# Two levels of seven products for queries and keys, over pairs of batches, with inner weight sums loaded for each pair

## The chip, the cores and the metric

The kernel runs on one core of one Trainium2 chip. The metric is the device time of one execution in microseconds. The core has five engines with a queue of instructions each: TensorE (PE in the profile, its weight loads PEld), VectorE (DVE), ScalarE (ACT), GpSimd (POOL) and SyncE (SP), which issues nearly all transfers. Each engine takes its instructions in order; between engines there are semaphores. 16 DMA engines carry the transfers. All data is fp32.

## The reference

For 64 batches of 256 tokens with 512 features, two layers are computed, each with a residual sum and a normalization over the features:

```python
deg = jnp.sum(adj, axis=-1, keepdims=True)
agg = jnp.einsum('bij,bjf->bif', adj, x) / jnp.maximum(deg, EPS)
out = relu(jnp.einsum('bnf,of->bno', concatenate([x, agg], axis=2), W))   # layer 0
x = _layernorm(x + out)

q, k, v = proj(Wq, bq), proj(Wk, bk), proj(Wv, bv)                         # layer 1, 8 heads of 64
scores = einsum('bhqd,bhkd->bhqk', q, k) * SCALE * (adj + adj)
ctx = einsum('bhqk,bhkd->bhqd', softmax(scores), v)
x = _layernorm(x + ctx @ Wo.T + bo)
```

The weights W are 512 x 1024, the four weights of layer 1 are 512 x 512.

## The kernel before

**Work and names.** The work of a batch is cut into small steps, each a function under a short name; a word such as `L35+2` in a plan means step L35 for batch 2i+2. The names that matter here:

- Dzx, xT: x is loaded in blocks and turned, features to partitions. xS: its sums for the outer level. Ls: sums for the inner level, in small tiles xs. L and Le: products of the first layer and what takes them out of PSUM.
- Dadj, Dza, aT, deg: the adjacency matrix, its turned copy, its row sums. Y, Yk, Yj: neighbours' product and its taking out. Dx, AYr, AYb, AYp, AYn: the rows of x, the residual sum, and the first normalization.
- Dway, Dz1, x1T, yS: the result goes through DRAM and comes back turned; sums of it. Q, V: queries and keys, values; Qk, Qj, Vk, Vj take them out.
- For each of four pairs of heads a to d: S (scores, two 64-row products side by side), m (mask and maximum), M, e, f (exponentials), r, n (normalize), T, Dw, Ds (turned on VectorE and through DRAM), C (context, two 64-column products side by side), c (copied).
- cS, O, Ok, Oj: output product and what takes it out. Drest, bo: the residual with bias. lb, lp, ln, Dout: the last normalization and the store.

**Seven products.** A product of two matrices cut in two each way is made of seven products of sums of blocks instead of eight (`winograd`, L461). Three accumulators a, b and c (banks of PSUM) collect them, and products are added onto what was already taken out. So of product 6 the sum goes onto product 1's bank after `k1` has read it. The first layer (L, `split_product`, L527) does this twice over: the outer level over a pair of batches, with seven outer products, each again of seven, 49 products of 128x256 for a pair. `W0_inner` holds the inner sums of the weights for good. Batches 0 and 1 use one level (P, `multiply_first`, L583). Queries and keys (`multiply_q`, L615) use one level for each batch: seven steps of eight products of 128x128. Values and output (`right_weights`, L498) use one level for each batch: seven steps of two products of 128x256. Neighbours (Y): seven of 128x256.

**Order.** START, PLAN and END list all steps over all engines, in an order that a planner made ahead of time; each engine takes its instructions in the order of these lists. PLAN is one turn, for two batches: it holds the first layer of batches 2i+2 to 2i+5 beside the second of 2i-1 to 2i+2. It is run 28 times. The SyncE queue follows the same list: a transfer whose buffer isn't free holds all behind it. PSUM has eight banks, given out in turn. One tile of 256 rows is held for `x`.

Of the kernel before, what the change touches and what calls it, by code (L numbers as in the profile page):

```python
# [22 lines left out]
LAST_TURNS = 2  # L23
START = """
    Dzx:0 W0h0:0 Dzx:1 W0h1:0 xT1:0 xT0:0 xS3:0 xS1:0 W0s1:0 P1:0 Dza:0 xT1:1 P5:0 xT0:1 xS1:1 Wo:0
    Pk5:0 P5:1 P1:1 Pk5:1 xS2:1 Pk1:0 xS2:0 Dadj:1 W0s2:0 P2:0 W0i1:0 Dzx:2 P6:0 aT:0 W0s3:0 Pk6:0 xS4:0
    Dadj:0 Pk1:1 aS1:0 W0s4:0 P7:0 Pj2:0 Dx:0 P3:0 Pj7:0 Y1:0 Pj3:0 Wb:0 P4:0 W0i5:0 bS1:0 bS3:0 Y5:0
    Pk4:0 xT0:2 aS3:0 P6:1 Dza:1 aS2:0 deg:0 xS3:1 Yk5:0 bS2:0 Yk1:0 Pk6:1 Wq:0 Y6:0 Y2:0 Yk6:0 aS4:0
    bv1:0 xS4:1 Y3:0 Yj2:0 bS4:0 Y7:0 Yj7:0 Yj3:0 Y4:0 AYr0:0 P7:1 AYb0:0 Yk4:0 AYp0:0 AYr1:0 P2:1 xT1:2
    AYn0:0 AYb1:0 P3:1 Pj7:1 AYp1:0 Pj2:1 Dzx:3 bv2:0 Pj3:1 AYn1:0 aT:1 Dway:0 aS1:1 P4:1 bv3:0 bS1:1  # L30
    Wv:0 deg:1 bS3:1 Y5:1 xS1:2 Pk4:1 W0i4:0 Y1:1 WqS:0 bS2:1 Y2:1 aS2:1 Yk1:1 xS3:2 Y6:1 aS4:1 Dz1:0
    xT0:3 xT1:3 Ls11:2 aS3:1 Yk5:1 Ls12:2 Yk6:1 Dx:1 Y3:1 xS1:3 Wqs1:0 L11:2 Ls51:2 Y7:1 Le11:2 bS4:1
    L51:2 Wqs3:0 L15:2 Ls13:2 L16:2 Ls52:2 L55:2 Yj7:1 Dza:2 Le16:2 Ls53:2 Wqs2:0 Le51:2 Wvs1:0 Y4:1
    L56:2 L17:2 x1T:0 Le56:2 Wvs2:0 L12:2 L52:2 L57:2 Yj3:1 yS1:0 Yk4:1 Q1:0 Dadj:2 Yj2:1 AYr0:1 V5:0
    Qk1:0 AYb0:1 Q5:0 Vk5:0 AYr1:1 AYp0:1 AYb1:1 V1:0 yS2:0 AYn0:1 aT:2 AYp1:1 W0i3:0 Qk5:0 Q6:0 Vk1:0  # L35
    Ls14:2 AYn1:1 yS3:0 Wqs4:0 V6:0 Le15:2 Dway:1 Qk6:0 L13:2 Le17:2 yS4:0 W0i2:0 Vk6:0 L14:2 Wvs4:0
    Le55:2 Q7:0 Le14:2 Le13:2 Ls23:2 Le57:2 Ls21:2 Le52:2 Ls22:2 L21:2 Le12:2 Ls54:2 Qj7:0 L54:2 Ls24:2
    V3:0 Le21:2 Le54:2 Wvs3:0 deg:2 Dx:2 L26:2 L53:2 Le26:2 Q4:0 xS2:3 W0i6:0 aS1:2 Dz1:1 xS2:2 Le53:2
    V7:0 Qk4:0 Ls61:2 Ls63:2 L25:2 Ls62:2 L61:2 Le25:2 Ls64:2 L27:2 Le61:2 xS3:3 Q2:0 Vj3:0 Drest:0
    Le27:2 W0i7:0 L22:2 L23:2 Qj2:0 L65:2 Ls71:2 Le23:2 L66:2 L62:2 Le66:2 L24:2 Le62:2 Q3:0 Vj7:0  # L40
    Le24:2 L67:2 V4:0 Le67:2 Le65:2 L64:2 Qj3:0 Vk4:0 L63:2 xS4:2 Le64:2 Le63:2 Sd:0 Ls72:2 Le22:2 xS4:3
    Sb:0 md:0 Ls31:2 Sc:0 La12:3 mb:0 Sa:0 La12:2 L75:2 L35:2 mc:0 Ls33:2 L71:2 Md:0 V2:0 Mb:0 fd:0
    Ls74:2 ma:0 L31:2 Mc:0 Ls32:2 eb:0 L72:2 L32:2 L41:2 Le75:2 ec:0 Ma:0 Dadj:3 Le71:2 Ls73:2 L73:2
    Le31:2 aS3:2 ed:0 x1T:1 Y1:2 Wos1:0 L76:2 L36:2 fb:0 Dzx:5 Le35:2 V1:1 Ls34:2 Le36:2 Le76:2 yS1:1
    fc:0 Le73:2 L33:2 rd:0 Le72:2 L37:2 nd:0 Le33:2 L77:2 La22:2 Le32:2 Dzx:4 Q1:1 Le77:2 rc:0 Le37:2
    bS1:2 Vj2:0 nc:0 Le41:2 Ls41:2 L74:2 Ls42:2 L34:2 Le74:2 Y5:2 ea:0 rb:0 Le34:2 La22:3 L46:2 Yk1:2
    L45:2 Tc:0 nb:0 Q5:1 bS2:2 aS2:2 Le45:2 Dwc:0 Le46:2 Ls44:2 fa:0 Yk5:2 V5:1 Ls43:2 Td:0 Qk1:1 L47:2
    yS2:1 Y6:2 Le47:2 Dwd:0 L42:2 yS3:1 Vk1:1 L44:2 Le42:2 bS3:2 Q6:1 ra:0 Yk6:2 na:0 aS4:2 Tb:0 Le44:2
    V6:1 Dwb:0 Vk5:1 Ta:0 Qk5:1 Dsc:0 V2:1 yS4:1 Vk6:1 xT0:5 Y7:2 bo:0 Qk6:1 L43:2 xT0:4 V3:1 Dwa:0
    xT1:5 Q7:1 Le43:2 Yj7:2 Vj3:1 bS4:2 Dsd:0 xT1:4 Ls13:4 V7:1 Wos2:0 Y4:2 Vj7:1 Y2:2 Yk4:2 bS1:3 Q3:1  # L50
    AYr1:2 Dsa:0 Wos4:0 deg:3 Y3:2 Qj7:1 Ls11:4 V4:1 xS3:4 AYb1:2 Dza:3 xS3:5 Q4:1 Vk4:1 Vj2:1 Qj3:1
    Wos3:0 Yj3:2 Yj2:2 Q2:1 Qk4:1 xS1:5 AYr0:2 Dsb:0 AYp1:2 AYb0:2 Qj2:1 C1a:0 AYp0:2 AYn1:2 C1b:0 xS1:4
    AYn0:2 Sd:1 c1:0 Dway:2 Sa:1 md:1 Sc:1 Sb:1 aT:3 Md:1 Ls53:4 fd:1 mc:1 Ls12:4 C0a:0 aS1:3 Ls51:4
    C0b:0 ma:1 Mc:1 Ls14:4 c0:0 Y5:3 Ls52:4 Y2:3 cS1:0 Dz1:2 mb:1 O2:0 aS2:3 cS3:0 O5:0 Yk5:3 aS3:3 Dx:3
    Y1:3 Ma:1 O1:0 Mb:1 Yk1:3 fa:1 cS2:0 L51:4 Ls54:4 Ok1:0 fb:1 L55:4 Ok5:0 bS2:3 O6:0 Yj2:3 Dza:4 ed:1
    L15:4 Ok6:0 cS4:0 Y6:3 Oj2:0 Le51:4 O7:0 ea:1 Yk6:3 aS4:3 x1T:2 bS4:3 L56:4 eb:1 Y3:3 bS3:3 O3:0
    Oj7:0 yS1:2 Yj3:3 Le56:4 ra:1 Y7:3 rb:1 na:1 L52:4 Yj7:3 V5:2 AYr0:3 Le52:4 O4:0 ec:1 Oj3:0 AYb0:3
    Y4:3 nb:1 L57:4 Yk4:3 AYp0:3 L11:4 AYr1:3 V1:2 AYb1:3 yS3:2 Q1:2 Vk1:2 Le11:4 rd:1 Ok4:0 AYp1:3
    AYn0:3 lb0:0 Q5:2 Tb:1 lp0:0 AYn1:3 Le15:4 aT:4 Le55:4 Dwb:1 Qk1:2 L13:4 yS2:2 Dadj:4 Le57:4 L16:4
    Ta:1 L54:4 Le16:4 V6:2 Le54:4 xS2:4 lb1:0 nd:1 Dway:3 L53:4 xS2:5 L17:4 Dwa:1 Le53:4 Ls63:4 L12:4  # L60
    Le17:4 Ls61:4 Q6:2 fc:1 Ls62:4 Ls23:4 Dsb:1 Vk6:2 Ls21:4 rc:1 Le12:4 Vk5:2 nc:1 Le13:4 L14:4 yS4:2
    L25:4 V7:2 Ls22:4 lp1:0 Le14:4 V3:2 Qk6:2 Vj7:2 Tc:1 Ls24:4 L21:4 Dz1:3 Qk5:2 Ls64:4 L61:4 Q7:2
    Le21:4 Td:1 ln1:0 ln0:0 Dwc:1 Le61:4 V4:2 Vj3:2 Dsa:1 Le25:4 L26:4 Qj7:2 Vk4:2 L65:4 Le26:4 V2:2
    Dwd:1 L27:4 Q4:2 Dsc:1 L23:4 Qk4:2 Q3:2 Le23:4 Le65:4 L66:4 Dsd:1 L63:4 Le66:4 L62:4 deg:4 L67:4
    Q2:2 Le27:4 Qj3:2 Dout:0 Le67:4 L24:4 x1T:3 L64:4 L22:4 xS4:5 Vj2:2 C0a:1 Le63:4 Ls71:4 Le62:4 xS4:4
    C0b:1 Le24:4 Le64:4 Ls31:4 Le22:4 C1a:1 Ls72:4 Qj2:2 Ls74:4 C1b:1 La12:4 c1:1 Sa:2 Ls32:4 c0:1
    Drest:1 Sb:2 ma:2 cS1:1 Dx:4 Sc:2 Ls33:4 cS3:1 mb:2 Sd:2 Ma:2 La12:5 fa:2 L75:4 L71:4 mc:2 L35:4
    Mb:2 Ls73:4 L72:4 eb:2 aS1:4 O5:1 Dzx:7 Le71:4 yS1:3 Le75:4 ea:2 O2:1 md:2 bo:1 L76:4 fb:2 L31:4
    L73:4 Dadj:5 Le31:4 O1:1 Le76:4 Le35:4 L36:4 aS3:4 Ok1:1 L77:4 Mc:2 ra:2 L32:4 Le72:4 cS2:1 na:2
    Dzx:6 Le77:4 L41:4 Ok5:1 Ls41:4 O6:1 Le73:4 Md:2 Ls34:4 rb:2 Le36:4 ec:2 Ta:2 cS4:1 L33:4 L37:4 ed:2  # L70
    La22:4 L45:4 Le32:4 Dwa:2 O3:1 Le33:4 Le37:4 nb:2 Ls43:4 Ok6:1 L74:4 bS1:4 L42:4 Le74:4 O7:1 Le41:4
    La22:5 fd:2 Oj2:1 Oj3:1 L34:4 Oj7:1 V5:3 fc:2 Ls42:4 Le45:4 Ls44:4 rd:2 lb0:1 Y1:4 nd:2 Y5:4 Dsa:2
    Yk1:4 L46:4 aS2:4 O4:1 yS3:3 Le46:4 Le34:4 Vk5:3 L47:4 rc:2 bS2:4 Le42:4 nc:2 V1:3 Tb:2 bS3:4 Q5:3
    Le47:4 Dwb:2 Vk1:3 Yk5:4 Ok4:1 Td:2 L44:4 yS2:3 Y6:4 Q1:3 lp0:1 xT1:7 Yk6:4 Tc:2 L43:4 Qk1:3 Y7:4
    xT0:7 Dwc:2 V6:3 Le43:4 Dwd:2 Yj7:4 Q6:3 bS4:4 Dza:5 Vk6:3 ln0:1 aS4:4 Y4:4 Qk6:3 yS4:3 Y2:4 Yk4:4
    V7:3 xS1:7 Le44:4 Qk5:3 Y3:4 Dsc:2 Q7:3 Yj3:4 AYr1:4 AYb1:4 Q3:3 Dsd:2 Vj7:3 Qj7:3 lb1:1 V2:3 xT1:6
    lp1:1 Q2:3 xT0:6 aT:5 Ls13:6 Dsb:2 ln1:1 AYp1:4 Yj2:4 Q4:3 AYr0:4 aS1:5 Qj3:3 AYn1:4 Dout:1 AYb0:4
    V3:3 Qk4:3 Qj2:3 AYp0:4 V4:3 Vj3:3 deg:5 Vk4:3 Ls11:6 Sd:3 AYn0:4 bS1:5 Vj2:3 C1a:2 Ls12:6 Dway:4
    Dza:6 C1b:2 C0a:2 c1:2 md:3 C0b:2 Drest:2 Md:3 c0:2 Sa:3 xS1:6 ed:3 aS3:5 Sb:3 ma:3 cS1:2 fd:3 Sc:3
    Dz1:4 Ls14:6 Ls51:6 mb:3 Y5:5 Ma:3 Ls52:6 Y1:5 ea:3 aS2:5 O2:2 bS2:5 Dx:5 Yk1:5 fa:3 O1:2 mc:3 Mb:3  # L80
    O5:2 bo:2 Y2:5 L51:6 Yj2:5 L11:6 Yk5:5 Y6:5 Le11:6 L55:6 Le51:6 cS2:2 Ok5:2 L16:6 Ok1:2 Mc:3 L52:6
    Yk6:5 bS3:5 ec:3 L56:6 x1T:4 aS4:5 Y7:5 bS4:5 fb:3 Y3:5 Yj7:5 yS1:4 O6:2 Yj3:5 Le16:6 eb:3 cS3:2
# [76 lines left out]
def kernel(  # L159
# [912 lines left out]
```

## Time and profile before

| | |
|---|---|
| runs | 2978.38, 2980.99, 2980.94 us; median 2980.94 |
| span of the profiled execution (the page gives no other time of it) | 2979.5 us |
| TensorE busy | 2948.7 us, 99% |
| VectorE, GpSimd, ScalarE busy | 2251.9, 1864.2, 1651.0 us |
| transfers | 510.77 MB, mean 171 GB/s |
| period of a turn, from L11 to L11 | 91.29 us |

A group line shows line, engine and operation, output and inputs, shapes and count, then busy time, the mean of one, and the idle time before with what ended it. Ends of matmuls are modelled, so TensorE's prices are read from start to start. The DMA share is the busy share of 16 engines.

### The profile page before, as it was taken

Reading aid. Unit: us, or ns where it says so; the run is one execution under the profiler, and the core shown is the slowest. Engines: PE = TensorE matmul, PEld = TensorE weight load, DVE = VectorE, ACT = ScalarE, POOL = GpSimd, SP = SyncE. Lnnn points to the kernel's source line nnn. Section 1 sums busy time; section 2 is a strip of 40 time slices with the busy share of each in tenths; the row PEclk is TensorE's granted clock in tenths of the full one; section 3 lists DMA queues with packets and bytes.
Section 4 is the critical chain, followed back from the end, with each engine's and each line's share of the span. In section 5 each row is a group of like instructions: output and inputs, shape, how many; then the busy total and the mean of one; then the engine's idle time right before and its main releaser. Section 6 shows DMA issues by size and latency. Waiting matters only on the chain.

```text
span 2979.5 us, 60265 instructions
## 1 busy us (share of the span) xinstructions
PE 2948.7 (99%) x18874; PEld 2576.7 (86%) x18874; DVE 2251.9 (76%) x6302; ACT 1651.0 (55%) x5001; POOL 1864.2 (63%) x3435
## 2 busy tenths in 40 slices
PE   7999999999999999999999999999999999999998
PEld 4888898888888888888888888888888888888886
DVE  6877777777787777777777877777777777777774
ACT  2455555555564555555655645656556556555565
POOL 5756666666566566666665665756666656657553
PEclk9999999999999999999999999999999999999999
DMA  7476666765756666667656577666676665776764
GB/s 173 125 190 179 165 173 155 199 179 156 187 159 174 188 173 168 172 159 194 180 157 185 159 181 188 166 175 167 156 198 176 165 180 153 192 183 164 178 171 116
DMA packets 492573, 510.77 MB, mean 171 GB/s; under 512 B 113760, under 2 KB 391264, under 8 KB 492256
## 3 DMA queue, kind: packets, MB, share of 16 engines
q1 hardware_dynamic: 490912, 505.87, 64.7%
q8 instruction: 153, 2.51, 0.4%
q14 instruction: 164, 1.34, 0.2%
q10 hardware_dynamic: 1344, 1.05, 0.2%
HBM read 307.50 MB, written 199.23 MB: 170 GB/s over the span
## 4 chain that ended last, share of the span: by engine, by line
PE 98%; POOL 1%; DVE 1%; DMA 0%; issue 0%; ACT 0%; SPq 0%; ACTq 0%; POOLq 0%; DVEq 0%
PE Qa L619 15%; PE pc L933 8%; PE Qc L619 8%; PE Va L501 7%; PE Oa L501 7%; PE Qb L619 4%; PE Vc L501 4%; PE Ya L708 4%; PE Oc L501 4%; PE Ycb L708 3%; PE sca L816 2%; PE scc L816 2%; PE scd L816 2%; PE scb L816 2%; PE Vb L501 2%; PE Ob L501 2%
## 5 line engine op out<-in xcount | busy, mean ns | idle before, releaser
L635 ACT ACTIVATE qk<-Qa,bqk 128x128 f32<-128x128 f32 x768 | 219.0, 370 | 281.5 <-PE Qa L619 281.5
L670 POOL TENSOR_SCALAR mv<-mv 128x1 f32<-128x1 f32 x256 | 67.2, 262 | 383.7 <-DVE mv L665 252.5
L619 PEld LDWEIGHTS Qa<-x1T,Wq 128*128 128x128 f32 x2048 | 248.6, 192 | 6.8 <-issue 0.3
L619 PE MATMUL Qa<-x1T,Wq 128*128 128x128 f32 x2048 | 249.4, 275 | 0.0
L989 ACT COPY cT<-pc 128x512 f32<-128x512 f32 x126 | 70.8, 586 | 250.5 <-PE pc L933 250.4
L676 ACT ACTIVATE rest<-rest,mv 128x512 f32<-128x512 f32 x128 | 100.8, 810 | 177.3 <-POOL mv L672 177.3
L832 DVE CUSTOM_DVE_ANT_0 sc<-scc,adj 128x256 f32<-128x256 f32 x256 | 92.5, 418 | 105.1 <-PE scc L816 103.1
L676 ACT ACTIVATE x<-oy,mv 128x512 f32<-128x512 f32 x128 | 105.4, 823 | 117.6 <-POOL mv L672 115.0
L440 POOL TENSOR_TENSOR xS<-xT,xS 128x256 f32<-128x256 f32 x64 | 47.1, 737 | 195.4 <-PE L6a L554 190.8
L851 ACT ACTIVATE sc<-sc,nmaxc 128x256 f32<-128x256 f32 x256 | 127.5, 500 | 71.7 <-DMA zx<-in_x_dram 39.7
L790 POOL TENSOR_TENSOR rest<-rest,bo_sb 128x512 f32<-128x512 f32 x128 | 160.7, 1277 | 8.5 <-DMA rest<-way 8.3
L851 ACT ACTIVATE sa<-sa,nmaxa 128x256 f32<-128x256 f32 x256 | 127.0, 497 | 68.5 <-POOL nmaxa L845 63.7
L671 POOL TENSOR_TENSOR mv<-mv,neg_half 128x1 f32<-128x1 f32 x256 | 144.8, 566 | 21.3
L875 ACT ACTIVATE sb<-sb,totalb 128x256 f32<-128x256 f32 x252 | 107.4, 498 | 78.9 <-DVE totalb L863 78.9
L832 DVE CUSTOM_DVE_ANT_0 sa<-sca,adj 128x256 f32<-128x256 f32 x256 | 93.2, 421 | 74.9 <-PE sca L816 72.1
L851 ACT ACTIVATE sb<-sb,nmaxb 128x256 f32<-128x256 f32 x256 | 127.8, 503 | 37.5 <-POOL nmaxb L845 37.5
L577 POOL TENSOR_TENSOR xs<-xS 128x128 f32<-128x128 f32 x248 | 113.0, 461 | 46.3 <-PE L5cb L554 38.5
L851 ACT ACTIVATE sd<-sd,nmaxd 128x256 f32<-128x256 f32 x256 | 126.8, 497 | 19.4 <-POOL nmaxd L845 19.4
L405 DVE STREAM_TRANSPOSE xT<-zx 128x512 f32<-128x512 f32 x128 | 89.0, 699 | 63.3 <-issue 55.8
L730 DVE SCALAR_TENSOR_TENSOR oy<-Ya,deg,oy 128x256 f32<-128x256 f32 x256 | 120.7, 471 | 20.8 <-PE Ya L708 17.2
L501 PE MATMUL Va<-Wv,x1T 128*128 128x256 f32 x512 | 131.6, 379 | 0.0
L501 PE MATMUL Oa<-Wo,cT 128*128 128x256 f32 x504 | 129.5, 379 | 0.6 <-DVE rest L657 0.6
(329 smaller groups left out, 9796.0 us busy)
## 6 DMA issues: line engine op xcount, KB each, us to landing
x<-in_x_dram SPq DMA_DIRECT2D x256, 128.0 KB, 3.9
way<-x SPq DMA_DIRECT2D x64, 512.0 KB, 2.8
z<-way SPq DMA_DIRECT2D x256, 128.0 KB, 3.2
rest<-way SPq DMA_DIRECT2D x64, 512.0 KB, 4.8
zx<-in_x_dram SPq DMA_DIRECT2D x254, 128.0 KB, 3.7
out_dram<-rest SPq DMA_DIRECT2D x254, 128.0 KB, 2.6
wsc<-sc SPq DMA_DIRECT2D x63, 512.0 KB, 3.4
wsd<-sd SPq DMA_DIRECT2D x63, 512.0 KB, 3.0
```

Source lines behind the costliest of these rows:

```text
L501: nc.tensor.matmul(ps[:, :width].rearrange("p (m o) -> p m o", o=G), lhsT=left(k, b, c), rhs=w(OUTER[k])[:, :, c], start=first and c == 0, ...
L619: nc.tensor.matmul(ps.rearrange("p (m j q) -> p m j q", m=2, j=2)[:, m, j], lhsT=wqk(OUTER[k])[:, m, c, j * P : (j + 1) * P], rhs=left_y(k ...
L635: nc.scalar.activation(part_q(b, t, n)[:, m, j], ps.rearrange("p (m j q) -> p m j q", m=2, j=2)[:, m, j], AF.Identity, bias=bqk[:, m, c : ...
L671: nc.gpsimd.tensor_tensor(mv[:, 1:2], mv[:, 1:2], neg_half, ALU.pow)
L676: nc.scalar.activation(dst, src, AF.Identity, bias=mv[:, 0:1], scale=mv[:, 1:2])
L708: nc.tensor.matmul(ps[:, G:] if acc == "b" else ps[:, :G], lhsT=left(b), rhs=right(b), start=k in (5, 1), stop=True, skip_group_check=True,)
L730: nc.vector.scalar_tensor_tensor(h, ps[:, G:] if acc == "b" else ps[:, :G], held["deg", b][:, t : t + 1], h, ALU.mult, ALU.add)
L790: nc.gpsimd.tensor_tensor(rest, rest, bo_sb, ALU.add)
L816: nc.tensor.matmul(sc(b, j)[:, t], lhsT=qk[d, 0, hp, t * P : (t + 1) * P], rhs=qk[d, 1, hp].rearrange("d (t b m) -> d b t m", t=NT, m=L), ...
L832: nc.vector.tensor_tensor_reduce(out=s[:, :, :, r], in0=sc(b, j)[:, t].rearrange("p (a c l) -> p a c l", a=A, l=L), in1=held["adj", b][:, ...
L851: nc.scalar.activation(rows(b)[:, r], rows(b)[:, r], AF.Exp, bias=of("nmax", b)[:, r : r + 1], accum_out=of("total", b)[:, r : r + 1],)
L933: nc.tensor.matmul(ps[j * D : (j + 1) * D, hp % 2], lhsT=held["v", b][:, c, h * D : (h + 1) * D], rhs=held[f"s{name}", b][:, :, c, j * NT ...
```

## The change

1. Queries and keys are computed for a pair of batches in two levels (steps H, `split_scores`), as the first layer is: 49 steps of two 128x128 products. GpSimd makes the inner sums Hs and the last sums Ha00, Ha12, Ha22. The outer level runs over batch and feature half; q and k are kept in half tiles, four buffers.
2. Values are computed for a pair in one level, seven steps of four products.
3. The inner weight sums of the first layer and of H, and three sums of Wv, are made once, stored to DRAM, and loaded again for each pair (Dwi, Dqi, Dvi) into three buffers.
4. Products 2 and 3 share a bank side by side and are taken out by one 512-wide instruction (L, H, Y, O). Some takings of L2 move to ScalarE, with a sum La00 on GpSimd.
5. The row sums of adj move from VectorE to ScalarE (deg, deh). The factors of a normalization are made for both token tiles at once (AYp, AYq, lp, lq).
6. x is loaded in two half tiles, Dx0 and Dx1, which share one buffer; the normalized rows are written to oy.
7. START, PLAN and END are new; PLAN is run 29 times.

```diff
-LAST_TURNS = 2
+LAST_TURNS = 1
+WI_BUFS = 3
+XS_BUFS = 3
+QK_BUFS = 4
+V_BUFS = 6
...
-    SPLIT = (1, 5, 2, 6, 7, 3, 4)
-    w0_inner = const.tile([P, len(SPLIT), 3, G], F32, name="W0_inner")
+    SPLIT = (1, 2, 5, 6, 7, 3, 4)
+
+    def inner_tile(of, k, b):
+        return part_of(f"wi{of}{k}", b, [P, 3, G], tag="wi", bufs=WI_BUFS)
...
+        @step(f"D{of or 'w'}i{k}")
+        def _(b):
+            nc.sync.dma_start(out=inner_tile(of, k, b), in_=held[f"wkept{of}{k}", 0])
...
+    def load_x(t):
+        @step(f"Dx{t}")
+        def _(b):
+            rows = tile_of(f"x{t}", b, [P, F], tag="x")
+            for a, part in groups():
+                nc.sync.dma_start(out=rows[part], in_=token_rows(x[b], a)[:, t])
...
-        nc.vector.tensor_reduce(deg, held["adj", b], AX.X, ALU.add)
+        for t in range(NT):
+            rows = held["adj", b][:, t]
+            nc.scalar.activation(rows, rows, AF.Identity, accum_out=deg[:, t : t + 1])
...
+        def product(q):
+            @step(f"H{k}{q}")
+            def _(b):
+                to = accumulator(q, b)
+                w = inner_weights("q", wqk_unit, k, b)[q]
+                for m in range(2):
                     nc.tensor.matmul(
-                        ps.rearrange("p (m j q) -> p m j q", m=2, j=2)[:, m, j],
-                        lhsT=wqk(OUTER[k])[:, m, c, j * P : (j + 1) * P],
-                        rhs=left_y(k, b, c),
-                        start=first and m == j == c == 0,
+                        to[:, m],
+                        lhsT=w[:, m],
+                        rhs=rights[q](b),
+                        start=q in (5, 1) and m == 0,
                         stop=True,
                         skip_group_check=True,
                     )
...
+                if q == 3:
+                    dst = qk_block(b, beta, n)[:, :, :, t * P : (t + 1) * P].rearrange("p m j q -> p j m q")
+                    ps = held[f"H{k}cb", b].rearrange("p (j m q) -> p j m q", j=2, m=2)
+                else:
+                    dst, ps = piece(n), accumulator(q, b)
+                if k in (1, 5) and q in (5, 1, 6, 4):
+                    bias = bqk_more if k == 5 else bqk[:, :, 2:]
+                    for m in range(2):
+                        nc.scalar.activation(dst[:, m], ps[:, m], AF.Identity, bias=bias[:, m, j : j + 1])
+                elif k == 2 and q in (5, 1, 6, 4):
+                    nc.scalar.copy(dst, ps)
+                else:
+                    nc.vector.tensor_tensor(dst, ps, dst, ALU.add)
...
+    @step("Ha12")
+    def _(b):
+        dst, one, two = qk_block(b, 0, 1), qk_block(b, 1, 0), qk_block(b, 1, 1)
+        for m in range(2):
+            nc.gpsimd.tensor_tensor(dst[:, m], one[:, m], two[:, m], ALU.add)
```

In the new PLAN these words stand around the first use of Dx1 and around the softmax of heads a (words of other steps are left out, the order is the list's; batches as the list counts them, so that a turn's H and S are those of -2):

```
... Sd-2 md-2 H62-2 Y3+0 H63-2 H67-2 Yj3+0 H71-2 He67-2 Y7+0 AYr0+0 H64-2 V2-2 Yj7+0 Dx1+0 AYb0+0 rd-2 He63-2
    Y4+0 He64-2 H35-2 Yk4+0 AYr1+0 V3-2 Td-2 AYb1+0 Dx0+1 H31-2 H75-2 Dwd-2 Dqi4-2 H32-2 He31-2 H72-2 H36-2 ...
... H74-2 Sa-2 H41-2 V4-2 ... H47-2 H43-2 Y1+1 He43-2 Ta-2 H44-2 C1a-2 C1b-2 Dwa-2 Dsb-2 Sd-1 Sc-1 Y6+1
    L26+2 Dsa-2 L16+2 Y7+1 Y3+1 L25+2 L22+2 Y4+1 Sb-1 Sa-1 C0a-2 C0b-2 ...
```

## The prediction

> **What bounds the kernel now.** I read the page's shares and chain first, then one pass of the plan (a "turn", two batches), then TensorE's timeline where its row rate changes, then transfers.
>
> ```profile
> PE 2948.7 (99%) x18874; PEld 2576.7 (86%) x18874; DVE 2251.9 (76%) x6302; ACT 1651.0 (55%) x5001; POOL 1864.2 (63%) x3435
> ...
> q1 hardware_dynamic: 490912, 505.87, 64.7%
> ...
> PE 98%; POOL 1%; DVE 1%; DMA 0%; issue 0%; ACT 0%; SPq 0%; ACTq 0%; POOLq 0%; DVEq 0%
> ```
>
> The chain is TensorE almost from end to end. The stretch view of one turn (columns: stretch, its length, then busy time of PE, PEld, DVE, ACT, POOL, granted clock, DMA share, GB/s) says the same of the middle:
>
> ```profile
> 963.50:1054.80 91.30, 91.30 (x591) 80.64 (x591) 69.91 (x197) 51.44 (x156) 58.29 (x109) 1.00 0.64 174
> ```
>
> In the timeline the product L11 starts every 91.29 us through the turns. So only TensorE's own work counts today, and VectorE has 21 us, GpSimd 33 us of slack a turn. The timeline gives the price of each product (start to start, since ends are modelled):
>
> ```profile
> 1038.68 1.03 PE L501 MATMUL Va<-Wv_sums,x1T 128*128 128x256 f32 x4
> 1039.54 1.95 PE L619 MATMUL Qc<-yS,Wq 128*128 128x128 f32 x16
> 1041.42 1.08 PE L933 MATMUL pc<-sc,v 128*64 128x256 f32 x8
> 1042.33 1.03 PE L933 MATMUL pc<-sa,v 128*64 128x256 f32 x8
> 1043.20 1.03 PE L933 MATMUL pc<-sb,v 128*64 128x256 f32 x8
> 1044.06 1.03 PE L933 MATMUL pc<-sd,v 128*64 128x256 f32 x8
> 1045.02 1.14 PE L816 MATMUL sca<-qk 64*128 64x256 f32 x8
> 1045.99 1.03 PE L816 MATMUL scd<-qk 64*128 64x256 f32 x8
> 1046.86 1.03 PE L816 MATMUL scb<-qk 64*128 64x256 f32 x8
> 1047.72 1.03 PE L816 MATMUL scc<-qk 64*128 64x256 f32 x8
> 1048.68 0.70 PE L708 MATMUL Ycb<-yB,aS 128*128 128x256 f32 x2
> 1049.21 0.59 PE L708 MATMUL Ya<-oy,aT 128*128 128x256 f32 x2
> 1049.65 1.03 PE L501 MATMUL Ob<-Wo,cT 128*128 128x256 f32 x4
> ```
>
> A 128x256 product is two instructions and takes 0.432 us (1049.65 to 1050.51 is two of them, 0.864). Q's step of eight 128x128 products takes 1.78, 0.223 each. S (64 rows) and C (64 columns) take 0.865 inside a run, but each change of shape costs about 0.1 before and 0.1 after it: 0.96 for the last C, 0.97 for the first S, 0.96 for the last S, 0.53 instead of 0.43 for the first Y. So a change costs 0.2 us (0.145 into C). The turn adds up: L 49 x 0.432 = 21.2; Y 14 x 0.432 = 6.05; V and O 56 x 0.432 = 24.2; Q 14 x 1.783 = 25.0; S and C 16 x 0.865 = 13.8; six changes 1.1. Sum 91.3, as measured: no wait is left in it.
>
> **The change, part by part: TensorE.** Q's 112 products of 128x128 a pair become H's 98 (49 steps of two): 98 x 0.223 = 21.85, 3.1 us less. V, O, Y and L keep their counts. But in the new order S stands alone four times and C and S form four more runs: 18 changes a turn instead of 6, 3.4 us instead of 1.1, so 2.3 of the 3.1 go back. Here the row leads, and the Trainium skill speaks against the change (TensorEngine Tiling (Array Packing), Key Properties: changing the tiling mode, not the tile within it, drains the engine). Without that rule I would write 88.2 a turn; with the row, **90.5**. Over the whole program, counted from both instruction orders: matmuls 2901.0 to 2801.1, changes 37.3 to 110.7, sum 2938.2 to 2911.8. What span holds beyond it today is 41.3 us (first loads 8 us, waits at both ends, closing work); I keep it. 2911.8 + 41.3 = **2953** with no new wait, against the span 2979.5 of this execution (median of the runs 2980.9, 1.4 more, which I ignore).
>
> **VectorE, GpSimd, ScalarE.** Means of rows overlap (a turn's sum of VectorE means is 82, its busy time 69.9), so I take start to start of instructions that stand back to back in the timeline: VectorE 0.33 for a 256-wide sum from PSUM (mean 0.42), 0.60 for a 512-wide, 0.39 for a Y part, 0.70 for AYr, 1.15 for the 128x1024 transpose, 0.1 for a tiny one; GpSimd 0.415 for 128x128, 0.69 for 256, 1.235 for 512. *VectorE:* H takes out 7 x 0.60 + 23 x 0.33 = 11.8 where Q took 6 x 0.60 = 3.6; L falls from 41 x 0.33 = 13.5 to the same 11.8; the degree sums leave (-1.2); merged Y and V parts -0.3; eight small norm steps +0.8. Sum +5.8: 75.7 a turn. *GpSimd:* Hs 28 x 0.415 = 11.6, Ha 6 and La00 2 x 1.235 = 9.9, norm factors 8 x 0.96 to 4 x 0.52 = -5.6, yS -0.7. Sum +15.2: 73.5. *ScalarE:* biases -2.9, V -0.2, L +1.1, degree sums +2: 51. All stay below 90, so I cost them at nothing, hidden behind TensorE. But the list bunches them: of 32 us of TensorE work from Yj7 on, VectorE has 33.3 listed, and GpSimd 32 of 34 across the turn's seam. Without cover the first alone is 1.3 a turn.
>
> **Transfers.** Fourteen loads of 384 KB and three of 256 KB a turn, 6.3 MB beside 16. By the packet records (0.117 us mean for 2 KB, 0.177 for 4 KB, so 0.147 for 3 KB): (14 x 128 x 0.147 + 3 x 128 x 0.117)/16 = 19.3 us of all 16 engines on 0.647 x 91.3 = 59, a share of 0.87. SP issues about 117 transfers instead of 92 at 0.45 each, 52 of 90 us. The trace has no 384 KB load; its neighbours are x's 128 KB at 3.9 and rest's 512 KB at 4.8, so about 4.4. Six loads are listed 4.1 to 4.8 us of TensorE work ahead of first use, Dvi4 and Dvi6 (256 KB) 3.0, the others 6 and more. The list's places are not times, so I take 0, hidden behind the products between; if these eight came 1 us late each it is 8 us a turn.
>
> **Two waits that the order makes.** Landing times (columns: transfer, KB each, median us to landing):
>
> ```profile
> x<-in_x_dram SPq DMA_DIRECT2D x256, 128.0 KB, 3.9
> wsa<-sa SPq DMA_DIRECT2D x63, 512.0 KB, 4.2
> sa<-wsa SPq DMA_DIRECT2D x252, 128.0 KB, 4.1
> adj<-in_adj_dram SPq DMA_DIRECT2D x256, 64.0 KB, 2.5
> ```
>
> *Wait A.* x now has one half-size buffer, so Dx1 can't be issued until AYr0 has read the other half, and AYr1 waits for it. Clock from the end of Y3. Sd ended at -1.0, md (4 x 0.42) runs from -0.85, then Yj3 0.70, an H6 sum 0.33, AYr0 0.70: done at 2.6. SP issues four at 0.45, the last at 4.0. Landing: 1.7 (adj's shortest in its tile view) to 3.9 (x's median); nearest in size is adj's 2.5, in row length x; I take 3.0, so 7.1 with latency. AYr1 ends at 7.8, and behind it stand Td 1.15, AYb1 0.8, He31 0.33: 10.2. H36 adds onto what He31 reads, so it waits. TensorE has from Y3 to H36 nine H-steps at 0.446, two Y at 0.432, two V at 1.73: 8.3. It is **1.9 us** late (0.6 to 2.8). The skill's fit (DMA: Bandwidth & Descriptors, Anatomy of one DMA — SWDGE (gpsimd) path: 2.0 us plus bytes over 436 GB/s) gives 2.15 for 64 KB and a wait of 1.05. It is for another issuing path, and x's shortest in the trace is 2.4 at 128 KB with a median of 3.9, so I stay by the rows. Late next: He71 and He35 on VectorE; and SP, where the next batch's Dx0 waits for AYr1 with Dwd, Dqi4 and Dsd behind it (H45 and C1b, which use them, are 13 us off).
>
> *Wait B.* After H43: He43 0.75 with its latency, Ta 1.15, Dwa 4.2, Dsa's fourth issue 1.35 and landing 4.1, latencies 0.2: 11.75 to C0a. TensorE has Y1, H44, C1a, C1b, Sd, Sc, seven L and Y, Y4, Sb, Sa there: 10.4 with changes. **1.3** (0 at the shortest landings, 2.6 each, to 3). Before, C0a stood at least 8.8 us behind Dsa alone.
>
> The two lie in different stretches of the turn and add: 90.5 + 3.2 = 93.7. Some 30 turns' worth x 3.2 = 96; 2953 + 96 = **3049**.
>
> **Rivals.** (1) *Faster: transfers land near their shortest.* Place: Dx1, Dwa, Dsa. A falls to 0.6 and B to 0: 2953 + 18 = 2971. It decides from A + B below 0.6 a turn for more than 0.2%. For it: in quiet quarters adj landed in 1.9. Against it: the share of 0.65 becomes 0.87. (2) *The DMA engines become late as a whole.* In the fullest quarter turn (share 0.95) zx and rest took 7.5 to land. Then A is 6 and loads stall: turn 96 to 98, some 3150. For it: the share; against: large packets. (3) *VectorE or GpSimd is the bound in its crowded stretch*: 1.3 excess plus 3 idle at AYr1, turn 94.8, about 3080. (4) *The change doesn't save products*: excluded, the built order has 98 products a pair.
>
> **How the numbers follow.** Waits A and B as sized: 0.53 (own range 3010 to 3085), and the likeliest. Rival 1: 0.24, of which 0.18 ends faster by more than 0.2% (about what a measurement of this kernel can tell from no change) and 0.06 within. Rival 3: 0.13. Rival 2: 0.10. So faster 0.18, same 0.06, slower 0.76. The range runs from 2953, the sum without any wait, to 3120, half way into rival 2; what it leaves out is most of rival 2 and an error in the prices themselves.
>
> **What would show it.** The turn's period at 93 to 94; S and C runs with 0.2 at each edge; AYr1 waiting for x's landing some 2 to 3 us and H3a's third product for He31; C0a waiting for sa. Wrong if the period is under 91.3, if AYr1 does not wait, or if the waits name wi or GpSimd's ys instead.

## The result and the profile after

The changed kernel takes 3163.05 us (median of four runs, 3150.88 to 3174.11), the kernel before 2980.97: the ratio is 1.0613, with an interval from 1.0586 to 1.0641. It is slower, as forecast, but by 182 us where 68 were forecast, and outside the range of the prediction. The profiled run took 3159.39 us, its span is 3157.5.

The page of the changed kernel, shares, transfer queue and chain:

```profile
PE 3001.4 (95%) x17978; PEld 2458.3 (78%) x17978; DVE 2531.7 (80%) x6727; ACT 1652.3 (52%) x4869; POOL 2390.8 (76%) x3817
...
q1 hardware_dynamic: 572768, 705.28, 73.5%
...
PE 56%; DMA 19%; DVE 12%; SPq 4%; POOL 4%; issue 3%; ACT 1%; DVEq 0%; ACTq 0%; POOLq 0%
```

Before, 98% of the chain was TensorE. Now 19% is transfers and 12% VectorE: TensorE waits in many places. The stretch view of one turn (columns as before: stretch, length, busy PE, PEld, DVE, ACT, POOL, clock, DMA share, GB/s):

```profile
919.00:1015.00 96.00, 91.79 (x561) 75.43 (x560) 76.94 (x208) 50.74 (x152) 74.02 (x121) 1.00 0.75 226
```

The turn's period was 91.29 throughout. Now, from L15 to L15, it is 95.99 on average and changes from turn to turn (94 to 99). TensorE's waits in the changed kernel (waited for: us in all, times, longest):

```profile
PE H3a L724 <- DVE qk L753: 40.7, 29, 2.0
PE H1cb L724 <- DMA wiq<-wkeptq: 14.0, 26, 1.3
PE H2a L724 <- DMA wiq<-wkeptq: 11.0, 12, 2.3
...
PE Va L784 <- DMA wiv<-wkeptv: 5.7, 9, 1.4
PE pc L1118 <- DMA sa<-wsa: 3.7, 8, 0.6
```

The first is H36, which waits for He31 once a turn (29 times): the place of wait A of the prediction. The next three are loads of inner weights, which the prediction had at nothing. The last is wait B. That waits name the loads was one of the prediction's own signs of being wrong.

This view leaves out short waits. To see them too, I took for each product the time to the next start, less its price and 0.1 for a change of shape on either side. In the steady turns this *excess* is 5.1 us a turn (before: under 0.6): H36 1.58, H26 0.67 and H15 0.65 (both first users of a load), V4 0.28, C0a 0.22, and some thirty places of 0.03 to 0.16. START (to 344 us, before to 324) and END have 60 to 70 us more of it than before, about 40 of them in START.

A part of the excess is TensorE's clock. In the changed kernel the profile shows a granted clock of 0.50 in twelve stretches of 3.4 or 6.8 us, 48 us in all; before there are three, 14 us in all. One of the twelve:

```profile
908.80:912.20 3.40, 3.40 (x18) 3.17 (x18) 2.72 (x6) 1.36 (x4) 1.01 (x3) 0.50 0.69 206
```

An H step takes 0.86 there instead of 0.445, so these stretches make at most 17 of the 182 us. Five lie in START and three in the last turn and END. The four others each begin within 1.2 us after the start of an H36 that had waited 2.1.

Landing in the changed kernel (transfer, KB each, median us):

```profile
wiq<-wkeptq SPq DMA_DIRECT2D x217, 384.0 KB, 4.4
wi<-wkept SPq DMA_DIRECT2D x210, 384.0 KB, 4.1
x<-in_x_dram SPq DMA_DIRECT2D x512, 64.0 KB, 2.3
zx<-in_x_dram SPq DMA_DIRECT2D x254, 128.0 KB, 5.4
...
wsa<-sa SPq DMA_DIRECT2D x63, 512.0 KB, 3.8
...
sa<-wsa SPq DMA_DIRECT2D x252, 128.0 KB, 3.4
```

And what SyncE's queue stands still for:

```profile
SPq L354 <- PE H5a L724: 149.8, 30, 6.0
...
SPq L474 <- DVE oy L937: 122.8, 65, 3.6
```

The load of 384 KB lands as estimated. But a Dvi load (L354) holds SyncE's queue 5 us a turn until H5 has freed its buffer, and Dx0 and Dx1 (L474) hold it 4 us a turn until AYr has read the other half of x: what is listed behind is issued late.

### The profile page after: what moved, and what is told of

Its sections match the earlier page's. It is cut to its first block, busy times and chain, and to the rows that moved or that the text cites. A ratio compares the mean times of both kernels' runs of the same rounds, so it can differ in the third digit from the quotient of the medians.

```text
span 3157.5 us, 61001 instructions
## 1 busy us (share of the span) xinstructions
PE 3001.4 (95%) x17978; PEld 2458.3 (78%) x17978; DVE 2531.7 (80%) x6727; ACT 1652.3 (52%) x4869; POOL 2390.8 (76%) x3817
## 3 DMA queue, kind: packets, MB, share of 16 engines
q14 instruction: 181, 1.48, 0.2%
q10 hardware_dynamic: 1344, 1.05, 0.1%
## 4 chain that ended last, share of the span: by engine, by line
PE 56%; DMA 19%; DVE 12%; SPq 4%; POOL 4%; issue 3%; ACT 1%; DVEq 0%; ACTq 0%; POOLq 0%
DMA wiq<-wkeptq 6%; PE Va L784 6%; PE Oa L810 5%; PE pc L1118 4%; PE Ocb L810 3%; PE Ya L897 2%; DVE oy L937 2%; DMA x<-in_x_dram 2%; PE Ycb L897 2%; PE scb L1001 2%; DVE oy L634 2%; PE scc L1001 2%; PE L4a L617 2%; PE H3a L724 2%; PE H4a L724 2%
## 5 line engine op out<-in xcount | busy, mean ns | idle before, releaser
L642 POOL TENSOR_TENSOR ys<-x1T 128x128 f32<-128x128 f32 x256 | 117.7, 461 | 139.2 <-PE L2cb L617 133.8
L1060 ACT ACTIVATE sc<-sc,totalc 128x256 f32<-128x256 f32 x252 | 107.4, 499 | 127.4 <-DVE totalc L1048 127.4
L749 ACT ACTIVATE qk<-H5a,bqk_more 128x128 f32<-128x128 f32 x192 | 59.5, 361 | 205.4 <-PE H5a L724 205.4
L828 DVE TENSOR_TENSOR rest<-Oa,rest 128x256 f32<-128x256 f32 x252 | 103.1, 409 | 58.6 <-PE Oa L810 57.0
L937 DVE SCALAR_TENSOR_TENSOR oy<-oy,x 128x512 f32<-128x512 f32 x128 | 110.6, 864 | 33.4 <-DMA x<-in_x_dram 33.1
L920 DVE SCALAR_TENSOR_TENSOR oy<-Ya,deg,oy 128x256 f32<-128x256 f32 x256 | 122.1, 477 | 16.5 <-PE Ya L897 15.5
L865 ACT ACTIVATE oy<-oy,mv 128x512 f32<-128x512 f32 x128 | 97.3, 807 | 72.8 <-DVE mv L858 72.6
L853 POOL TENSOR_TENSOR mv<-mv,neg_half 128x2 f32<-128x2 f32 x128 | 91.7, 716 | 47.1 <-DVE mv L847 41.6
L1060 ACT ACTIVATE sd<-sd,totald 128x256 f32<-128x256 f32 x252 | 107.5, 497 | 35.5 <-DVE totald L1048 35.5
L1060 ACT ACTIVATE sa<-sa,totala 128x256 f32<-128x256 f32 x252 | 107.3, 501 | 27.7 <-DVE totala L1048 27.7
L1017 DVE CUSTOM_DVE_ANT_0 sd<-scd,adj 128x256 f32<-128x256 f32 x256 | 93.3, 421 | 29.1 <-PE scd L1001 28.9
```

What stands on the lines that cost most here:

```text
L865: nc.scalar.activation(dst, src, AF.Identity, bias=mv[:, 0:1], scale=mv[:, 1:2])
L920: nc.vector.scalar_tensor_tensor(h, ps[:, part], held["deg", b][:, t : t + 1], h, ALU.mult, ALU.add)
L937: nc.vector.scalar_tensor_tensor(h, h, 0.0, held[f"x{t}", b], ALU.max, ALU.add)
L1060: nc.scalar.activation(dst, src, AF.Identity, scale=of("total", b)[:, r : r + 1])
```

## The experiments

All times are medians of four runs. `noload` and its kin compute other values for Q, K, V and the first layer, so their times are those of a kernel with the loads for free, not of a candidate. The runs with x2 in their names also add a row of Wo in the place of the output bias, and those with noha copy one term of Ha12 instead of adding two.

### Is wait A what the prediction says: x2 and order_a

```diff
-            rows = tile_of(f"x{t}", b, [P, F], tag="x")
+            rows = tile_of(f"x{t}", b, [P, F], tag=f"x{t}")
```

> The changed kernel with a buffer of its own for each half of x, so that Dx1 no longer waits for AYr0 (to make room, the bias row that step bo adds is replaced by a row of Wo; same instructions, other values). Theory 1 (wait A is one of two main causes of the steady loss): H36 stands 1.6 us late in each turn of the changed kernel; without it 29 x 1.6 = 46 us go, and the time is 3163 - 46 = 3117 (3100 to 3130). Theory 2 (VectorE and GpSimd are what TensorE waits for in that stretch, whichever buffer comes first): the next wait takes its place, 3150 to 3165. Theory 3 (the loads of inner weights alone): 3160 or more.

Measured: 3155.5 (3153.4 to 3167.2), within the spread of the changed kernel and in the range of theory 2. H36 still waits 1.57 a turn. x hardly lands earlier than it did: 5.8 us after the end of Y3, on average, for 6.1. In these traces nearly every transfer of SyncE is issued only when the transfer eight places before it in the queue has landed. Dx1 no longer waits for AYr0, but now stands behind a load of inner weights (L472 is Dx):

```profile
SPq L472 <- DMA wiq<-wkeptq: 46.9, 48, 1.7
```

order_a leaves the buffer alone:

```diff
-    ... Yk4+0 AYr1+0 Ha12-2 V3-2 fc-2 Td-2 AYb1+0 Dx0+1 H31-2 ... H36-2 He35-2 AYp+0 ...
+    ... Yk4+0 Ha12-2 V3-2 fc-2 Td-2 H31-2 ... H36-2 He35-2 AYr1+0 AYb1+0 Dx0+1 AYp+0 ...
```

> The changed kernel with one edit of the order: AYr1 and AYb1 of the turn's first batch (and the Dx0 behind them) are listed after He35 instead of before Td, so that VectorE is free for He31 while x is on its way; x keeps its one buffer. Theory 1 (wait A reaches TensorE through VectorE's queue): H36 no longer stands late, and about as much is won as with two buffers, 3110 to 3135. Theory 2 (VectorE has too much work there): the two instructions cost the same wherever they stand, 3150 to 3170. A loss above 3170 would say that the later Dx0 holds SP's queue and with it the loads behind.

Measured: 3156.2 (3138.0 to 3162.8). The wait has only moved, from H36 to H37 (1.35 a turn). Theory 1 falls in both: with the named cause gone, or passed by, something else holds the products as long. What that is, "Two causes beside each other" shows.

### What is there without the loads: noload_x2 and noload

```diff
         @step(f"D{of or 'w'}i{k}")
         def _(b):
-            nc.sync.dma_start(out=inner_tile(of, k, b), in_=held[f"wkept{of}{k}", 0])
+            loaded.add((of, k, b))
```

The products of a set that is in `loaded` read W0_sums instead; Dvi is changed in the same way, and x2's edit is in.

> The changed kernel with two buffers for x and with none of the loads of inner weights (Dwi, Dqi, Dvi): all products that used a loaded sum read one constant tile instead, so that the values of Q, K, V and the first layer are others, the instructions of TensorE, VectorE, ScalarE and GpSimd the same (and the bias row is a row of Wo). Theory 1 (x's buffer and the loads make all the waits): the sum of TensorE's own work, 2953, holds: 2950 to 2985. Theory 2 (VectorE and GpSimd bound in crowded stretches, with 77.6 and 74.7 us of a turn of 96): a third or more of the loss stays, 3020 to 3100.

Measured: 3064.1 (ratio to before 1.0286, 1.0271 to 1.0302). Theory 2 holds: the loads make about half of the loss, and the time without them is 111 us above TensorE's own sum. The turn is steady again, 92.72 in most turns. The excess is 2.6 a turn, of which H36 has 1.15, without any load.

> As noload_x2 (no loads of inner weights, one constant tile in their place), but with the one buffer for x that the changed kernel has, and the true bias row. Theory 1 (wait A was sized right in itself, and only hidden behind the loads): H36 stands later by the 1.1 us of the prediction's A beyond VectorE's own work, 29 x 1 = 30 us more than noload_x2: 3085 to 3100. Theory 2 (VectorE's own work sets H36, and x lands early enough once the engines are quieter): 3060 to 3072.

Measured: 3079.6, between the two ranges. x's one buffer costs 15.5 us here, half of what theory 1 has.

### Waiting for weights, or traffic: unread_x2 and thin_x2

In unread_x2 the loads are issued as they were, and `loaded.add` follows each, so that no product reads them. In thin_x2 each carries an eighth of its rows as well:

```diff
-            nc.sync.dma_start(out=inner_tile(of, k, b), in_=held[f"wkept{of}{k}", 0])
+            nc.sync.dma_start(out=inner_tile(of, k, b)[:16], in_=held[f"wkept{of}{k}", 0][:16])
```

> As noload_x2, but the loads of inner weights are issued and carried as in the changed kernel, into the same three buffers, only no product reads them: the traffic and SP's issues stay, no product waits for a load, and a load waits only for the load before it in its buffer. Theory 1 (products stand still for their own late weights): as without loads, 3060 to 3080. Theory 2 (half of it is what the traffic does to the other transfers, x, rest, sa and the rest): 3100 to 3115. Theory 3 (all of it is traffic): 3140 to 3155.

> unread_x2 with each load of inner weights cut from 128 rows to 16 (48 KB instead of 384, 32 instead of 256): SP issues as many transfers in the same places, the DMA engines carry an eighth of the bytes, and no product reads them. Theory 1 (the 61 us between noload_x2 and unread_x2 are the DMA engines' time): 3064 to 3075. Theory 2 (they are SP's issues and a queue that stands while a load waits for its buffer): 3110 to 3125.

Measured: unread_x2 3124.9, between theories 2 and 3; thin_x2 3071.0, theory 1. So of the 91 us between x2 and noload_x2, 54 go with the bytes on the DMA engines and 7 with SyncE's issues. The 31 between x2 and unread_x2 go with the products' wait for their own weights (H15 and H26 lose 1.3 us a turn), but not with that alone: a load that nobody reads need not wait for H5 to free its buffer either. In unread_x2 TensorE waits for other transfers:

```profile
PE H3a L735 <- DVE qk L764: 41.2, 30, 2.0
PE pc L1129 <- DMA sb<-wsb: 15.2, 19, 2.1
...
PE pc L1129 <- DMA sa<-wsa: 7.7, 11, 2.0
```

C0a in the middle of the turn and C0b at its end wait for sa and sb: 0.41 and 0.57 us a turn in the excess. C0a's is wait B. C0b's is a wait of the same kind that the prediction did not size. In the changed kernel they are 0.22 and nothing: there H15, shortly before C0b, waits for its load, and sb lands meanwhile. Without traffic (noload_x2) C0a's is 0.07.

The excess also tells where the 54 us go. Between unread_x2 and thin_x2 it differs by 1.55 us a turn: 0.54 at C0b, 0.43 at H36, 0.30 at C0a. The transfers of sa and sb land no later (medians 3.4 and 3.6, in thin_x2 3.6 and 3.6). What lands later is the stores ahead of them, wsa and wsb (3.7 and 3.8 against 2.9 and 2.9), and x, which SyncE issues later.

### The same traffic in the old order: before_loads

```diff
+    @step("Dnot")
+    def _(b):
...
+        load = sb.tile([P, 3, G], F32, tag="not", name=f"not_{len(spare)}", bufs=3)
+        spare[len(spare)] = load
+        width = G
+        nc.sync.dma_start(out=load[:, :, :width], in_=spare["kept"][:, :, :width])
```

> The kernel before with seventeen loads of 384 KB a turn added on SyncE's queue, evenly spaced, into three spare buffers that nothing reads; to make room, three of the seven inner sums of the first layer's weights are not made and other ones are read in their place (same instructions in every turn, other values). The DMA share rises as far as in the changed kernel. Theory 1 (6 MB more a turn cost only where a transfer's lead is short, and before's leads are long): 2975 to 2990. Theory 2 (that traffic costs by itself, as the 61 us between noload_x2 and unread_x2): 3025 to 3050.

Measured: 3003.2 (ratio 1.0085, 1.0068 to 1.0102), between the two theories. The page and the transfers of this kernel:

```profile
q1 hardware_dynamic: 559600, 693.47, 86.1%
...
not<-kept SPq DMA_DIRECT2D x476, 384.0 KB, 5.0
...
sa<-wsa SPq DMA_DIRECT2D x252, 128.0 KB, 4.9
sb<-wsb SPq DMA_DIRECT2D x252, 128.0 KB, 5.0
```

Its TensorE waits:

```profile
PE pc L948 <- DMA sb<-wsb: 9.2, 16, 1.1
...
PE pc L948 <- DMA sa<-wsa: 5.7, 9, 1.1
```

At a share even higher than the changed kernel's, sa and sb land about 1 us later than before (4.1 and 3.8), and the waits for them in this view come to 15 us in all. So the traffic has a price of its own, 25 us here. That the rest of the 54 comes from the shorter leads of the new order is likely but not settled, since these loads stand evenly spaced and those of the change do not.

### What is left without loads: noload_x2_late, noload_x2_noha, noload_x2_nosums

In one turn of noload_x2, VectorE from the end of Sd's maxima to He31, and GpSimd beside it (AYr is L946, Ha12 L782, He31 the last line of VectorE):

```profile
964.75 0.75 DVE L929 SCALAR_TENSOR_TENSOR oy<-Ycb,deg,oy 128x512 f32<-128x512 f32 x1
...
969.41 1.48 DVE L946 SCALAR_TENSOR_TENSOR oy<-oy,x 128x512 f32<-128x512 f32 x1
970.81 1.23 DVE L1074 STREAM_TRANSPOSE sd<-sd 128x1024 f32<-128x1024 f32 x1
971.97 0.65 DVE L852 BATCH_NORM_STATS2 stats<-oy 128x6 f32<-128x512 f32 x1
972.65 0.18 DVE L854 BATCH_NORM_AGGREGATE mv<-stats 128x2 f32<-128x6 f32 x1
972.87 0.42 DVE L856 TENSOR_SCALAR mv<-mv 128x2 f32<-128x2 f32 x1
973.20 0.41 DVE L762 TENSOR_TENSOR qk<-H3a,qk 128x256 f32<-128x256 f32 x1
```

```profile
969.06 2.96 POOL L782 TENSOR_TENSOR qk<-qk,qk 128x512 f32<-128x512 f32 x2 [0.55 <-DVE qk L762]
```

No line of VectorE in this stretch has an idle time before it, and TensorE waits for it. But AYr1 (969.41) takes 1.48 where a quiet one takes 0.66 to 0.70, and Ha12, which runs on GpSimd at the same time, takes 2.96 where it takes 2.50 in other turns. The first of Ha12's two sums ends at 970.34, and AYr1 ends 0.55 later. This is no chance: in the traces of the changed kernel, x2 and noload_x2 there are 72 AYr that begin while a GpSimd sum of 128x512 still has 0.25 us or more to run, and each ends 0.55 us after that sum, however long before it began. So AYr1 does not run slower, it stands until the sum is done.

Three runs take this apart. noload_x2_late lists AYr1, AYb1 and AYp behind He37:

> noload_x2 with one edit of the order: AYr1, AYb1 and AYp of the turn's first batch are listed after He37 instead of around Td, behind the takings of the H3 products. Theory 1 (those two stand in VectorE's queue ahead of He31, 1.15 us a turn): H36 no longer waits: 29 x 1.15 = 33 us less, 3031 (3025 to 3042). Theory 2 (VectorE has no idle time in the whole stretch, so a later product waits instead): 3055 to 3070.

Measured: 3069.7, theory 2. Now H74 waits for He77:

```profile
PE H7a L733 <- DVE qk L762: 30.2, 30, 1.0
```

noload_x2_noha takes Ha12 from GpSimd:

```diff
-            nc.gpsimd.tensor_tensor(dst[:, m], one[:, m], two[:, m], ALU.add)
+            nc.scalar.copy(dst[:, m], one[:, m])
```

> noload_x2 with the sum Ha12 left out on GpSimd (ScalarE copies one of its two terms instead, so that K and Q of one block are others). In noload_x2 Ha12 ran beside AYr1; AYr1 took 1.48 us instead of the 0.70 of a quiet one, Ha12 2.96 instead of 2 x 1.235. Theory 1 (the two slow each other down, and AYr1's 0.75 us is on TensorE's path through He31): 29 x 0.75 = 22 us less, 3042 (3036 to 3050). Theory 2 (AYr1's length is its own, or not on the path): 3060 to 3066.

Measured: 3036.7, 27 us less and in the range of theory 1. AYr1 takes 0.69, and H36's excess is 0.13. noload_x2_nosums makes no inner sums in START:

```diff
-        @step(f"W{of or 0}i{k}")
-        def _(b):
-            w = inner_weights(of, unit, k, b)
-            for dst, a, c in ((5, 7, 1), (6, 3, 5), (7, 3, 7), (4, 2, 6)):
-                engine.tensor_tensor(w[dst], w[a], w[c], ALU.subtract)
...
+        steps[f"W{of or 0}i{k}"] = steps[f"D{of or 'w'}o{k}"] = lambda b: loaded.add((of, k, b))
```

> noload_x2 without the inner sums of the weights that START makes once on VectorE (fourteen times four subtractions of 128x256) and without their stores; all products that would use them read the same constant tile. Theory 1 (these sums fill VectorE in START, where TensorE stood 33 us more than before's 11): 15 to 25 us less, 3040 to 3050. Theory 2 (START is slow for its order and its takings): 3058 to 3064.

Measured: 3045.4, 19 us less, theory 1. In the profiled executions it is 13 us, all of it won before the third L15.

### Two causes beside each other: noha and x2_noha

> The changed kernel, loads and all, with the sum Ha12 left out on GpSimd as in noload_x2_noha (ScalarE copies one of its two terms; K and Q of one block are others). Theory 1 (AYr1 beside Ha12 is on TensorE's path here too): 0.75 to 0.95 us a turn less, 3163 - 27 = 3136 (3130 to 3145). Theory 2 (with the loads there x lands late and AYr1 waits for it, or another wait takes the place): 3150 to 3165.

> The changed kernel, loads and all, with both edits: a buffer of its own for each half of x, and Ha12 left out on GpSimd (ScalarE copies one of its terms). Each edit alone gave next to nothing with the loads there (7.5 us less and 7 us more). Theory 1 (two causes stand side by side ahead of He31, x's buffer and AYr1 beside Ha12, and either alone is enough to hold H36 as long): together they give what wait A was costed at, 1.2 to 1.6 us a turn, 3163 - 40 = 3123 (3112 to 3130). Theory 2 (under the loads' traffic x lands late in any case, and the loads take up what is won): 3145 to 3160.

Measured: noha 3170.0 (3160.8 to 3180.6), x2_noha 3130.5 (3127.1 to 3142.1), which is half a microsecond above the range of theory 1 and far from theory 2. Each edit alone moves nothing beyond the spread, both together 32 us: more than the two changes added up. One turn of the changed kernel and one of x2 show why (AYr is L937 and L935, Ha12 L773 and L771, Yk4 the line ahead of AYr1, He31 the last). Changed kernel:

```profile
996.88 1.06 DVE L937 SCALAR_TENSOR_TENSOR oy<-oy,x 128x512 f32<-128x512 f32 x1
...
1000.03 0.47 DVE L920 SCALAR_TENSOR_TENSOR oy<-Ya,deg,oy 128x256 f32<-128x256 f32 x1
1002.38 0.87 DVE L937 SCALAR_TENSOR_TENSOR oy<-oy,x 128x512 f32<-128x512 f32 x1 [1.87 <-DMA x<-in_x_dram]
...
1005.30 0.42 DVE L753 TENSOR_TENSOR qk<-H3a,qk 128x256 f32<-128x256 f32 x1
```

```profile
1000.20 2.50 POOL L773 TENSOR_TENSOR qk<-qk,qk 128x512 f32<-128x512 f32 x2 [0.54 <-DVE qk L753]
```

x2:

```profile
999.56 0.47 DVE L918 SCALAR_TENSOR_TENSOR oy<-Ya,deg,oy 128x256 f32<-128x256 f32 x1
1000.96 1.81 DVE L935 SCALAR_TENSOR_TENSOR oy<-oy,x 128x512 f32<-128x512 f32 x1 [0.93 <-DMA x<-in_x_dram]
...
1004.83 0.42 DVE L751 TENSOR_TENSOR qk<-H3a,qk 128x256 f32<-128x256 f32 x1
```

```profile
999.72 2.50 POOL L771 TENSOR_TENSOR qk<-qk,qk 128x512 f32<-128x512 f32 x2 [0.56 <-DVE qk L751]
```

In the changed kernel AYr1 waits 1.87 for x, starts when Ha12 is nearly done, and takes 0.87. In x2 it waits 0.93, starts with Ha12's second sum, and takes 1.81. Both end 0.55 us after Ha12, and from the end of Yk4 to He31 it is 4.8 either way. What an earlier x wins is lost again while AYr1 stands for GpSimd.

The other turns say the same. H36's wait in the changed kernel has only two lengths, 1.1 us in 16 of the 29 turns and 2.1 in 13: AYr1 ends behind Ha12's first sum, or behind its second when x lands too late for the first. x2 has the same 16 and 13; noload_x2 has 1.1 in all 29. Without Ha12 the wait follows x's landing: in noha it lies anywhere from 0.8 to 2.1, with a mean of 1.12. That is 0.46 less than in the changed kernel, but C0a waits 0.41 more in that run. In x2_noha H36 keeps 0.90 a turn, since x still lands late under the loads.

### The price of a change of shape: before_spread and grouped

```diff
-    ... Sd+1 ma+1 cS1+0 Sb+1 Ls51+4 Dz1+2 md+1 Sc+1 Ma+1 bo+0 fa+1 Y5+3 Y1+3 mb+1 ...
+    ... Sd+1 ma+1 cS1+0 Ls51+4 Dz1+2 md+1 Ma+1 bo+0 fa+1 Y5+3 Sb+1 Y1+3 Sc+1 mb+1 ...
```

> The kernel before with one edit of the order: four of the S steps of a turn are moved behind one to three 128x256 products of Y or L, so that eight more changes of shape (64 rows to 128 and back) fall in a turn; no instruction is added. Theory 1 (a change of shape costs TensorE 0.2 us, as the prediction has it): 28 x 8 x 0.2 = 45 us more, 3026 (3015 to 3035). Theory 2 (the change is hidden behind the next weight load): 2981, within 5.

(Sd and Sb of the turn's other batch are moved likewise, behind L35 and L75.) Measured: 3030.2 (ratio 1.0174, 1.0157 to 1.0191), with a period of 93.13, steady: 1.84 us a turn more. Not all of it is the eight changes. One is a new wait of L35, which now follows Sa at once and whose sum Ls31 is not yet there:

```profile
PE L3cb L554 <- POOL xs L577: 4.8, 27, 0.2
```

From start to start L35 comes 0.25 late. What is left is 1.6 us, 0.20 for each change, the prediction's price. The reverse in the changed kernel, grouped (Sc next to Sd, Sb next to Sa):

> The changed kernel with one edit of the order: Sc stands next to Sd and Sb next to Sa (with m, M and e behind them), so that a turn has 14 changes of shape instead of 18; every step is done. Theory 1 (TensorE's own work is on the path, at 0.23 us a change by before_spread): 29 x 4 x 0.23 = 27 us less, 3136 (3130 to 3145). Theory 2 (in those stretches TensorE waits for VectorE and loads, so what it saves it waits): 3155 to 3165; later maxima that crowd VectorE would make it slower, 3165 to 3180.

Measured: 3266.5 (ratio 1.0963), 103 us more, and outside every range that was written down. TensorE's waits in grouped:

```profile
PE H4a L725 <- DVE qk L754: 37.8, 29, 1.6
PE scd L1002 <- DVE nmaxc L1018: 27.7, 29, 1.0
PE H3a L725 <- DVE qk L754: 23.0, 29, 1.6
```

Sd now waits for Sc's maxima (mc), and the products H wait for takings that stand later on VectorE. Four changes saved are 0.8 us a turn; the period rises to 99.6.

## Why the prediction was right or wrong

**What bounds the kernel; TensorE's own turn (90.5): right.** 95.99 less the excess of 5.1 is 90.9, within 0.4. The products of H show as priced (a step 0.445), and the change of shape costs the 0.2 that it was taken at. The Trainium skill's rule that a change of the tiling mode drains TensorE (TensorEngine Tiling (Array Packing), Key Properties) pointed the right way; the price itself came from the row.

**VectorE and GpSimd "I cost them at nothing, hidden behind TensorE": the sums right, the step wrong.** 77 and 74 a turn were forecast within 2. But in the stretch from Sd to He37 VectorE has no pause, so TensorE is not a cover there; and AYr was priced at 0.70 from a quiet row, where beside Ha12 it stands until GpSimd's sum is done, up to 1.8. Without loads this is 27 us. Rival 3 named the stretch, at 1.3 a turn, but not that one engine stands for the other.

**Transfers "I take 0, hidden behind the products between": the step that failed most.** The landing of 4.4 was right. What failed is that a lead in the list was taken for a lead in time. SyncE's queue stands still for Dvi and Dx and for loads that have not landed, and with 6 MB more a turn the stores wsa and wsb and the rows of x come late. Measured: 91 us between x2 and noload_x2, 31 of them with the loads' own users and 54 with the bytes. The prediction's "1 us late each" for eight loads would have been 8 a turn; the excess at the loads' users is 1.6, and the rest of the price is paid by other transfers. The share was forecast at 0.87 and is 0.75 in the turn shown. What the loads add was sized right, about 0.2, but the 59 us under it were carried over from before: without the loads the new kernel's transfers take 56.9% of the 16 engines where before had 64.7%.

**Wait A (1.9, range 0.6 to 2.8): right as a wait, wrong in its terms and as a cost; that 1.58 lies so near is in part luck.** In the turn shown AYr0 ends 2.5 us after Y3 (forecast 2.6), AYr1 starts at 7.0 (7.1), He31 is done at 10.3 (10.2), and H36 waits 1.94. But this is one of the 13 late turns. The landing was taken at 3.0 and has a median of 2.3; the prediction's other estimate, 2.15 by the Trainium skill's fit for another issuing path (DMA: Bandwidth & Descriptors, Anatomy of one DMA — SWDGE (gpsimd) path), was nearer, and its wait of 1.05 is close to the 1.12 that noha has with x alone as the cause. What fills the gap to 1.58 is Ha12, which the prediction did not have. And what is won by taking the named cause away is 7.5 us, within the spread, not 46: the sum counted one cause as if it stood alone.

**Wait B (1.3): right as a place, too large.** It is 0.22 in the changed kernel and 0.41 in unread_x2. The step that failed is the two landings: 4.2 for Dwa and 4.1 for Dsa were the medians of before, and in the changed kernel they are 3.8 and 3.4, 1.1 us less together, nearly the whole wait. That wait B and the others simply add did not hold either: C0b's wait at the turn's end goes when H15 waits ahead of it.

**The ends: "What span holds beyond it today is 41.3 us; I keep it": wrong.** START's and END's excess is 60 to 70 us more than before; the forecast's thirty turns' worth had some 13 of it. 13 to 19 us are VectorE's inner sums in START. The rest of START, and END, were not taken apart; without loads END's excess is 10 to 16 us smaller.

So of the 114 us between forecast and result about 60 are the 26 steady turns (96.0 instead of 93.7), about 55 the ends. Rival 2, the DMA engines late as a whole, named the nearest time (3150) with 1 chance in 10, but not the place: it has zx and rest late, and TensorE's waits name neither.

No kernel here beats the one before. Even with the loads for free and Ha12 gone, the changed one takes 3036.7 and is slower.

## What to carry to other kernels

A wait that the trace names is worth its length only if nothing of the same length stands beside it: before costing its removal, put the instruction where it would then run and see what it meets on the other engines. Loads that are added to a queue in order are to be judged by what that queue stands for and by what the new bytes do to the transfers with the shortest leads, not by their own landing. A saving on the engine that is the bound (here 0.8 us of 91 a turn by the prices) is soon spent when two other engines become 80 and 76% busy and hold it in turn.

## What was not expected of the hardware

A VectorE sum of 128x512 out of two SBUF tiles (AYr) takes 0.66 to 0.70 alone. When it begins beside a GpSimd sum of 128x512 it ends 0.55 us after that sum, in all 72 cases, and so takes up to 1.81; GpSimd's next sum can then stand for it in turn (2.96 for two instead of 2.50). Takings from PSUM beside GpSimd's sums keep their 0.41. A change between 64-row or 64-column products and full ones costs TensorE 0.20 us, in the rows of both kernels and in before_spread. SyncE's transfers stand for the one eight places before them, so that a load of 384 KB, 4 to 5 us on its way, delays what is issued behind it. And 17 loads of 384 KB a turn that nothing reads cost a kernel that was 99% TensorE 0.85%.
